# A third, SBUF-resident decay buffer for a selective scan, with decays made two parts ahead

## The chip, the cores and the metric

The kernel runs on one core of a Trainium2 chip. The metric is device time in microseconds (us) from the first to the last instruction of one launch; lower is better. Engines are named as in the profile: PE (TensorE matmul), PEld (its weight loads), DVE (VectorE), ACT (ScalarE), POOL (GpSimd), SP (SyncE, which issues almost all DMA here).

## The reference: what is computed

Input `x` is 8 images of 256 channels by 48x48 = 2304 positions, all float32. Two layers, each a residual on a group-normalised input.

Layer 0 compares all positions of an image: `pos` is normalised per position, `sim = pos @ pos.T`, the 16 largest similarities of each row go through a softmax, and the result is the weighted sum of the features of those 16 positions.

Layer 1 applies a selective-scan block twice (depth `d` = 0, 1), 512 channels by 16 states, over the 2304 positions in order:

```python
def step(h, inp):
    dt_t, B_t, C_t, x_t = inp
    dA = jnp.exp(dt_t[:, :, None] * A)
    h = h * dA + dt_t[:, :, None] * B_t[:, None, :] * x_t[:, :, None]
    y = jnp.einsum('bds,bs->bd', h, C_t)
    return (h, y)
```

`dA` is what this text calls a **decay**: one number per channel, state and position.

## The kernel before

Positions are cut in 6 chunks of T = 384. A **unit** is one chunk of one image at one depth: 8 x 6 x 2 = 96 units. A unit has 16 **steps**; a step covers 32 channels with their 16 states, laid out as 128 partitions by 4 state columns. A step has 2 **parts** of 2 states each. So there are 96 x 16 x 2 = 3072 parts, numbered `m`, and everything in the main loop hangs on that number. A part takes about 3 us.

For each part, in this order of the program:

- `carry(m - 1)` (L859, ACT) copies the last column of the previous part's states out to `h_st`, where that part was not one of POOL's.
- `decay` (L828, ACT) makes decays: two Exp instructions, 128x385 each (one column of zeros to restart the scan, then 384 positions), into the buffer that `decays(m)` names.
- on even parts, `make_bx(n + 2)` (L804, POOL) multiplies `BC` and `dtxr` into `bx` for the step two ahead, 128x1536; `pool_part(n - 1)` (L871, POOL) multiplies the states of the last step by C, for those parts that the table `SHARE` gives to POOL; `take_up` (ACT, or a memset of POOL) puts the carried states in `bx`.
- the hooks of the lists `between` and `behind`: projections, loads, normalisation of the units around this one. Each has a part number, relative to its unit, at which it is put into the queues. `load_in` (L590) loads one 128 KB tile `inw` of the input projection's weights, used by `in_proj` (L602) of the same number.
- `run_scan(m)` (L843, DVE) is one scan instruction over 770 columns. Its first input is the decays, its second is `bx`. Where POOL does the multiplication by C (part marked G in `SHARE`), the states are written over `bx`; where DVE does it, they are written over the decays, and a DVE multiply (L845) then takes decays and `BC` to `bx`.
- `sum_states` (L889, PE) later sums `bx` over the states into `y`.

Layer 0 of the next image runs interleaved with the scan, one slice of work a part (`ahead.go(m)`): similarity matmuls, DVE's top-16 (four instructions of about 2.5 us a block of 128 rows), ACT's exponentials into tiles `aT`, and at the end of a block `average` (L472) into `o`, with the residual `xr` loaded beside it (L474). Layer 0 of the first image runs alone, ahead of everything.

The order on each engine is the order of the program: it is written by hand, and each engine works its queue strictly in order. Waits are semaphores between engines.

The decay buffers of the kernel before are two PSUM tiles of two banks each. [...]

```python
    def decays(m):
        return banks[m % 2][:, 511 - T : 513 + T]
...
        carry(m - 1)
        decay(m + 1)
```

Of the kernel before, what the change touches and what calls it, by code (L numbers as in the profile page):

```python
# [8 lines left out]
F32 = mybir.dt.float32  # L9
# [6 lines left out]
P = 128  # L16
# [9 lines left out]
def tile_conv_preact(  # L26
# [19 lines left out]
    B, C, N = x.shape  # L46
# [4 lines left out]
    CB = C // P  # L51
    DB = DI // P
    NB = N // P
    T = 384
# [6 lines left out]
    HQ = 2  # L61
# [168 lines left out]
    def layer0(b, left, pool, ps0, alone):  # L230
# [3 lines left out]
        more = 2 if alone else 1  # L234
# [233 lines left out]

        def average(t):
            row = blocks[t]  # L470
            row["o"] = pool.tile([P, C], F32, tag="o", name=f"o_{b}_{t}", bufs=more)
            nc.scalar.activation(row["o"], row["po"], AF.Identity, scale=row["den"])  # L472
            row["xr"] = pool.tile([P, CB, P], F32, tag="xr", name=f"xr_{b}_{t}", bufs=more)
            nc.sync.dma_start(  # L474
                row["xr"], x[b, :, t * P : (t + 1) * P].rearrange("(k p) t -> p k t", p=P)
            )
# [9 lines left out]
        def finish(t):  # L486
# [15 lines left out]
            (-5, similar, 4), (-8, keep_similar, 0), (-5, keep_similar, 2), (24, turn_back), (18, weigh, 1),  # L502
            (17, weigh, 0), (1, top, 1), (-9, similar, 0), (-8, similar, 1), (-7, similar, 2),
            (22, average), (-6, similar, 3), (-7, keep_similar, 1), (-3, keep_similar, 3), (0, top, 0),
            (-3, keep_similar, 4), (15, turn, 1), (10, others, 4), (5, others, 0), (3, top, 2),
            (6, add_top), (11, invert), (5, others, 2), (17, turn, 2), (20, turn, 3),
# [18 lines left out]
    with tc.tile_pool(name="first", bufs=1) as pool0, tc.tile_pool(  # L525
        name="first_ps", bufs=1, space=PSUM
# [7 lines left out]
    with tc.tile_pool(name="setup", bufs=2) as setup:  # L534
        for d in range(DEPTH):
            for t in range(DC, DC + 1):
                dg = setup.tile([P, DB, P], F32, tag="dg", name=f"dg_{d}_{t}")
                for k in range(DB):
                    f = cw[:, d, k, t : t + 1] if t < DC else dpar[:, d, k : k + 1]
# [3 lines left out]
    keep = ctx.enter_context(tc.tile_pool(name="keep", bufs=2))  # L543
# [8 lines left out]
        nc.vector.memset(t[:, 0:1], NEVER)  # L552
    banks = [ps.tile([P, 1024], F32, tag=f"da{i}", name=f"da_{i}", bufs=1) for i in range(2)]

    def decays(m):
        return banks[m % 2][:, 511 - T : 513 + T]

    def mm(w, name):
        return ps.tile([P, 512], F32, tag="mm", name=name, bufs=3)[:, :w]
# [28 lines left out]
        unit["BC"].append(t)  # L588

    def load_in(unit, e):  # L590
        t = keep.tile([P, CB, P], F32, tag="inw", name=f"inw_{unit['u']}_{e}", bufs=4)
        nc.sync.dma_start(
            t, in_wT[unit["d"]].rearrange("(k p) e -> p k e", p=P)[:, :, e * P : (e + 1) * P]
        )
        unit["inw"][e] = t
# [168 lines left out]
    def silu_z(unit):  # L764
# [3 lines left out]
        for e in range(DB - 1):  # L768
# [11 lines left out]
             dt=[], dt_d={}, dtx_d={}, dtr={}, dtxr={}, bx={}, y={}, inw={}, dmat={}, taps={}, xi={}, cv={},  # L780
# [7 lines left out]
    def at(n):  # L788

        return units[n // STEPS], n % STEPS, n % STEPS // J  # L790
# [6 lines left out]
    def make_bx(n):  # L797


        if not 0 <= n < NSTEP:  # L800
            return
        unit, i, k = at(n)
        bx = keep.tile([P, Q, 1 + T], F32, tag="bx", name=f"bx_{n}", bufs=8)
        nc.gpsimd.tensor_tensor(  # L804
            bx[:, :, 1:], unit["BC"][0],
            unit["dtxr"][i].unsqueeze(1).to_broadcast([P, Q, T]), ALU.mult,
        )
        unit["bx"][i] = bx

    def take_up(n):  # L810

        if not 0 <= n < NSTEP:
            return
        unit, i, k = at(n)
        if unit["c"] == 0:
            nc.gpsimd.memset(unit["bx"][i][:, :, 0], 0.0)
        else:
            nc.scalar.copy(unit["bx"][i][:, :, 0], h_st[:, unit["d"], i])

    def decay(m):  # L820

        n, p = divmod(m, PARTS)
        if not 0 <= n < NSTEP:
            return
        unit, i, k = at(n)
        da = decays(m)
        for s in range(HQ):
            nc.scalar.activation(  # L828
                da[:, s * (1 + T) : (s + 1) * (1 + T)], unit["dtr"][i],
                AF.Exp, scale=A_sb[:, unit["d"], i, p * HQ + s : p * HQ + s + 1],  # L830
            )

    def run_scan(m):
        n, p = divmod(m, PARTS)
        if not 0 <= n < NSTEP:
            return
        unit, i, k = at(n)
        qs = slice(p * HQ, (p + 1) * HQ)
        bx = unit["bx"][i][:, qs]
        g = bx.rearrange("p q t -> p (q t)")  # L840
        da = decays(m)
        h = g if on_pool(unit, i, p) else da
        nc.vector.tensor_tensor_scan(h, da, g, 0.0, ALU.mult, ALU.add)  # L843
        if h is da:
            nc.vector.tensor_tensor(  # L845
                bx[:, :, 0:T], da.rearrange("p (q t) -> p q t", q=HQ)[:, :, 1:],
                unit["BC"][1][:, qs], ALU.mult,
            )

    def carry(m):  # L850

        n, p = divmod(m, PARTS)
        if not 0 <= n < NSTEP:
            return
        unit, i, k = at(n)
        if not on_pool(unit, i, p):
            h = decays(m).rearrange("p (q t) -> p q t", q=HQ)
            if unit["c"] + 1 < NCH:
                nc.scalar.copy(h_st[:, unit["d"], i, p * HQ : (p + 1) * HQ], h[:, :, T])  # L859

    def pool_part(n):

        if not 0 <= n < NSTEP:
            return
        unit, i, k = at(n)
        lo = [p for p in range(PARTS) if on_pool(unit, i, p)]
        if not lo:
            return
        qs = slice(lo[0] * HQ, (lo[-1] + 1) * HQ)
        g = unit["bx"][i][:, qs]  # L870
        nc.gpsimd.tensor_tensor(g[:, :, 0:T], g[:, :, 1:], unit["BC"][1][:, qs], ALU.mult)  # L871

    def carry_pool(n):

        if not 0 <= n < NSTEP:
            return
        unit, i, k = at(n)
        lo = [p for p in range(PARTS) if on_pool(unit, i, p)]
        if lo and unit["c"] + 1 < NCH:
            qs = slice(lo[0] * HQ, (lo[-1] + 1) * HQ)  # L880
            nc.scalar.copy(h_st[:, unit["d"], i, qs], unit["bx"][i][:, qs, T])
# [30 lines left out]
    def leave(unit, cb):  # L912
# [20 lines left out]
        (17, load_d, 2), (-17, tap, 1), (18, load_rep, "dtx", 13), (-8, times_x, 1), (19, gate, 1),  # L933
        (-22, normal), (1, load_rep, "dt", 3), (0, load_rep, "dtx", 4), (15, load_rep, "dt", 10), (6, load_rep, "dtx", 7),
        (10, load_rep, "dtx", 9), (12, load_rep, "dtx", 10), (20, load_rep, "dtx", 14), (11, gate, 0), (-29, spread_root),
        (-19, load_in, 5), (33, load_out), (-22, load_in, 0), (21, load_rep, "dt", 13), (-20, tap, 0),
        (-10, step_size, 1), (9, copy_z, 2), (-18, in_proj, 2), (2, load_rep, "dtx", 5), (10, sum_states, 0),
        (13, load_rep, "dt", 9), (29, gate, 2), (9, silu_z), (7, load_rep, "dt", 6), (19, load_rep, "dt", 12),
        (-6, load_rep, "dtx", 1), (-14, load_in, 7), (-30, root), (9, load_rep, "dt", 7), (4, load_d, 1),
        (-24, load_in, 3), (17, load_rep, "dt", 11), (14, load_rep, "dtx", 11), (-13, x_proj), (-17, load_in, 6),  # L940
        (-3, load_d, 0), (4, load_rep, "dtx", 6), (-4, load_rep, "dtx", 2), (-42, load_v),
    ]
    behind = [
# [1 line left out]
        (-8, load_rep, "dtx", 0), (-15, tap, 3), (-1, load_rep, "dt", 2), (-28, scale), (16, load_rep, "dtx", 12),  # L945
        (11, load_rep, "dt", 8), (8, in_proj, 6), (17, sum_states, 1), (-14, silu_x), (25, load_rep, "dt", 15),
        (-37, affine), (1, times_x, 2), (7, copy_z, 0), (8, load_rep, "dtx", 8), (-17, tap, 2),
        (-10, softplus), (-16, in_proj, 3), (3, load_rep, "dt", 4), (-29, load_in, 2), (6, in_proj, 7),
        (35, gate, 3), (-2, load_rep, "dtx", 3), (8, copy_z, 1), (40, leave, 1), (-3, times_x, 3),
        (22, load_rep, "dtx", 15), (-16, load_in, 4), (29, load_d, 3), (-37, mean), (-19, taps, 0),  # L950
        (-19, in_proj, 1), (-10, load_bc, 0), (33, sum_states, 3), (-30, root_end), (-9, times_x, 0),
        (-22, load_in, 1),
    ]
    inner, outer = {}, {}
    for w, unit in enumerate(units):
# [35 lines left out]
    for m in range(first, PARTS * NSTEP - HOOKS + last + 1):  # L991
        n, p = divmod(m, PARTS)
        carry(m - 1)
        decay(m + 1)
        if p == 0:
            make_bx(n + LEAD)
            pool_part(n - 1)
            take_up(n + 1)
        else:
            carry_pool(n - 1)  # L1000
        for f, unit, args in inner.get(m, ()):
            if f is load_v:
                ahead.finish(unit["b"])
            f(unit, *args)
        run_scan(m)
        for f, unit, args in outer.get(m, ()):
            f(unit, *args)
        ahead.go(m)
# [41 lines left out]
```

## Time and profile before

The time before is 9903.8 us (median of 2 runs, 9897.2 to 9910.4). The profiled execution spans 9897.1 us.

| engine | busy, us | share of the span | instructions |
|---|---|---|---|
| PE | 8000.3 | 81% | 36736 |
| DVE | 8956.8 | 90% | 7993 |
| ACT | 7322.2 | 74% | 15966 |
| POOL | 8943.3 | 90% | 3927 |

Read it in two stretches. In the first 515 us layer 0 of the first image runs alone: POOL is busy for 24.6 us of it and DVE for 242.4. In the rest, 9382 us, the scan runs with everything beside it, with DVE and POOL both busy for over nine tenths of each slice. A group's row gives the line, the engine, the output and inputs by name, the tile sizes, the count, then the busy time in us and the mean of one in ns, and last the idle time of the engine just before such an instruction with what ended it.

### The profile page before, as it was taken

Reading aid. Unit: us, or ns where it says so; the run is one execution under the profiler, and the core shown is the slowest. Engines: PE = TensorE matmul, PEld = TensorE weight load, DVE = VectorE, ACT = ScalarE, POOL = GpSimd, SP = SyncE. Lnnn points to the kernel's source line nnn. Section 1 sums busy time; section 2 is a strip of 40 time slices with the busy share of each in tenths; the row PEclk is TensorE's granted clock in tenths of the full one; section 3 lists DMA queues with packets and bytes.
Section 4 is the critical chain, followed back from the end, with each engine's and each line's share of the span. In section 5 each row is a group of like instructions: output and inputs, shape, how many; then the busy total and the mean of one; then the engine's idle time right before and its main releaser. Section 6 shows DMA issues by size and latency. Waiting matters only on the chain. (4 is left out here: it accounts for less than half of the span.)

```text
span 9897.1 us, 133780 instructions
## 1 busy us (share of the span) xinstructions
PE 8000.3 (81%) x36736; PEld 4388.5 (44%) x36736; DVE 8956.8 (90%) x7993; ACT 7322.2 (74%) x15966; POOL 8943.3 (90%) x3927
## 2 busy tenths in 40 slices
PE   8878887788878888788877888778887788866665
PEld 6644544444534454445444445344544444522222
DVE  4589998999989999899998999899998999988998
ACT  4477777778777877777877787777787778766766
POOL 0099999999989999899998999999998999999999
PEclk9989998899989998899988999889998899977777
DMA  1144445444444444444454444444445444444544
GB/s 32 37 133 126 134 130 152 124 132 129 136 142 131 129 134 137 140 126 133 130 148 128 130 128 134 144 132 125 135 128 152 121 133 127 138 136 129 145 138 122
DMA packets 1243503, 1271.37 MB, mean 128 GB/s; under 512 B 266592, under 2 KB 1215840, under 8 KB 1242752
## 3 DMA queue, kind: packets, MB, share of 16 engines
q1 hardware_dynamic: 1230496, 1262.45, 44.7%
q8 instruction: 293, 4.80, 0.2%
q14 instruction: 458, 3.75, 0.1%
q10 hardware_dynamic: 12256, 0.36, 0.1%
HBM read 1048.94 MB, written 212.86 MB: 127 GB/s over the span
## 5 line engine op out<-in xcount | busy, mean ns | idle before, releaser
L804 POOL TENSOR_TENSOR bx<-BC,dtxr 128x1536 f32<-128x1536 f32 x1536 | 5298.4, 3453 | 115.6 <-PE y L889 59.8
L828 ACT ACTIVATE da<-dtr,A_sb 128x385 f32<-128x385 f32 x6144 | 3591.0, 585 | 871.6 <-DVE bx L843 558.0
L843 DVE TENSOR_TENSOR_SCAN bx<-da,bx 128x770 f32<-128x770 f32 x2040 | 3521.8, 1746 | 190.5 <-ACT da L828 151.4
L871 POOL TENSOR_TENSOR bx<-bx,BC 128x1536 f32<-128x1536 f32 (+1 forms) x1320 | 3303.6, 2503 | 217.5 <-DVE bx L843 205.4
L843 DVE TENSOR_TENSOR_SCAN da<-da,bx 128x770 f32<-128x770 f32 x1032 | 1808.8, 1753 | 193.4 <-ACT da L828 149.0
L602 PE MATMUL pe<-vn,inw 128*128 128x384 f32 (+1 forms) x3072 | 1258.9, 543 | 394.1 <-DVE xr L924 87.0
L399 PE MATMUL psim<-pos 128*128 128x512 f32 (+1 forms) x2880 | 1370.8, 608 | 183.5 <-ACT sim L408 74.7
L465 PE MATMUL po<-feat,aT 128*128 128x256 f32 x5184 | 1364.0, 412 | 13.8 <-ACT aT L454 7.6
L889 PE MATMUL y<-bx,sel 128*32 128x384 f32 x12288 | 1221.2, 533 | 44.2 <-POOL bx L871 37.9
L465 PEld LDWEIGHTS po<-feat,aT 128*128 128x128 f32 x5184 | 1029.8, 205 | 361.9 <-issue 113.9
L845 DVE TENSOR_TENSOR bx<-da,BC 128x768 f32<-128x768 f32 x1032 | 988.8, 958 | 35.5
L602 PEld LDWEIGHTS pe<-vn,inw 128*128 128x128 f32 x3072 | 590.1, 206 | 902.6 <-issue 191.2
L399 PEld LDWEIGHTS psim<-pos 128*128 128x128 f32 x2880 | 552.8, 206 | 818.8 <-issue 470.8
L889 PEld LDWEIGHTS y<-bx,sel 128*32 128x32 f32 x12288 | 394.1, 118 | 856.6 <-issue 725.0
L702 DVE SCALAR_TENSOR_TENSOR xc<-pe,cw,xc 128x384 f32<-128x384 f32 x1152 | 695.7, 611 | 42.8 <-ACT xc L694 15.7
L732 PE MATMUL pd<-dbl,dtp_sb 16*128 16x384 f32 x768 | 424.3, 668 | 342.0 <-ACT dt L741 209.0
L859 ACT COPY h_st<-da 128x2 f32<-128x2 f32 x832 | 131.7, 158 | 686.4 <-DVE bx L845 680.0
L454 ACT ACTIVATE aT<-pt 128x512 f32<-128x512 f32 (+1 forms) x720 | 388.1, 548 | 245.9 <-PE pt L446 239.8
L445 PE MATMUL pt<-ident,sim 128*128 128x128 f32 x2592 | 539.6, 291 | 33.7 <-DVE v L666 17.6
L907 PE MATMUL pw<-z,ow 128*128 128x384 f32 x1536 | 531.5, 499 | 15.0 <-DVE v L666 7.0
L437 ACT ACTIVATE rest<-left,three 128x512 bf16<-128x512 f32 (+1 forms) x720 | 467.0, 670 | 59.7 <-DVE left L422 59.7
L446 PE MATMUL pt<-minus,rest 128*128 128x128 bf16 x2592 | 491.6, 225 | 3.2 <-ACT rest L437 3.2
(146 smaller groups left out, 9766.8 us busy)
## 6 DMA issues: line engine op xcount, KB each, us to landing
dtxr<-dtx_d SPq DMA_DIRECT2D x6144, 48.0 KB, 1.8
dtr<-dt_d SPq DMA_DIRECT2D x6144, 48.0 KB, 1.8
BC<-bc_d SPq DMA_DIRECT2D x768, 192.0 KB, 3.7
inw<-in_in_wT_dram SPq DMA_DIRECT2D x768, 128.0 KB, 2.2
dtx_d<-dtx SPq DMA_DIRECT2D x384, 192.0 KB, 2.0
dt_d<-dt SPq DMA_DIRECT2D x384, 192.0 KB, 2.2
ow<-in_out_wT_dram SPq DMA_DIRECT2D x96, 512.0 KB, 4.0
dmat<-diag SPq DMA_DIRECT2D x384, 64.0 KB, 2.3
```

The lines of the kernel that those rows point to most:

```text
L399: nc.tensor.matmul(pm, pos[:, k, t * P : (t + 1) * P], pos[:, k, c0 : c0 + w], start=(k == 0), stop=(k == CB - 1),)
L445: nc.tensor.transpose(pt[:, q], row["sim"][:, r], ident)
L465: nc.tensor.matmul(row["po"], aT[:, m % PT, :], feat[:, m, :], start=(m == 0), stop=(m == NB - 1))
L602: nc.tensor.matmul(pe, w[:, k], unit["vn"][:, k, lo:], start=(k == 0), stop=(k == CB - 1))
L702: nc.vector.scalar_tensor_tensor(unit["xc"][e], unit["pe"][e][:, k : k + T], cw[:, unit["d"], e, k : k + 1], unit["xc"][e], ALU.mult, ALU.add,
L804: nc.gpsimd.tensor_tensor(bx[:, :, 1:], unit["BC"][0], unit["dtxr"][i].unsqueeze(1).to_broadcast([P, Q, T]), ALU.mult,)
L828: nc.scalar.activation(da[:, s * (1 + T) : (s + 1) * (1 + T)], unit["dtr"][i], AF.Exp, scale=A_sb[:, unit["d"], i, p * HQ + s : p * HQ + s ...
L843: nc.vector.tensor_tensor_scan(h, da, g, 0.0, ALU.mult, ALU.add)
L845: nc.vector.tensor_tensor(bx[:, :, 0:T], da.rearrange("p (q t) -> p q t", q=HQ)[:, :, 1:], unit["BC"][1][:, qs], ALU.mult,)
L871: nc.gpsimd.tensor_tensor(g[:, :, 0:T], g[:, :, 1:], unit["BC"][1][:, qs], ALU.mult)
L889: nc.tensor.matmul(y[j * G : (j + 1) * G, :], sel, unit["bx"][k * J + j][:, q, 0:T], start=False, stop=True, skip_group_check=True,)
L907: nc.tensor.matmul(pw, unit["ow"][:, k, cb * P : (cb + 1) * P], unit["z"][k], start=(k == 0), stop=(k == DB - 1),)
```

## The change

The scan gets a third decay buffer. PSUM is full, so it is an SBUF tile, `room`, of 128 x 770 float32 = 3080 bytes a partition. Parts with `m % 3 == 2` use it; the others use the two PSUM buffers as before. With three buffers ACT makes the decays of part `m + 2` in part `m`, where it made those of `m + 1`.

The room for it comes from three places, 1 KB a partition each: layer 0's tiles `o` and `xr` lose their own buffers and take turns with `aT`, and `inw` has 3 buffers where it had 4. The part numbers of six of the eight `load_in` hooks (all but 4 and 7) are set anew for that.

```diff
-            row["o"] = pool.tile([P, C], F32, tag="o", name=f"o_{b}_{t}", bufs=more)
+            row["o"] = pool.tile([P, C], F32, tag="aT", name=f"o_{b}_{t}", bufs=2 * more)
...
-            row["xr"] = pool.tile([P, CB, P], F32, tag="xr", name=f"xr_{b}_{t}", bufs=more)
+            row["xr"] = pool.tile([P, CB, P], F32, tag="aT", name=f"xr_{b}_{t}", bufs=2 * more)
...
+    room = keep.tile([P, HQ * (1 + T)], F32, tag="room", name="room", bufs=1)
+
     def decays(m):
-        return banks[m % 2][:, 511 - T : 513 + T]
+        return room if m % 3 == 2 else banks[m % 3][:, 511 - T : 513 + T]
...
-        t = keep.tile([P, CB, P], F32, tag="inw", name=f"inw_{unit['u']}_{e}", bufs=4)
+        t = keep.tile([P, CB, P], F32, tag="inw", name=f"inw_{unit['u']}_{e}", bufs=3)
...
-        (-19, load_in, 5), (33, load_out), (-22, load_in, 0), (21, load_rep, "dt", 13), (-20, tap, 0),
+        (-15, load_in, 5), (33, load_out), (-22, load_in, 2), (21, load_rep, "dt", 13), (-20, tap, 0),
...
-        (-24, load_in, 3), (17, load_rep, "dt", 11), (14, load_rep, "dtx", 11), (-13, x_proj), (-17, load_in, 6),
+        (-24, load_in, 1), (17, load_rep, "dt", 11), (14, load_rep, "dtx", 11), (-13, x_proj), (4, load_in, 6),
...
-        (-10, softplus), (-16, in_proj, 3), (3, load_rep, "dt", 4), (-29, load_in, 2), (6, in_proj, 7),
+        (-10, softplus), (-16, in_proj, 3), (3, load_rep, "dt", 4), (-29, load_in, 0), (6, in_proj, 7),
...
-        (-22, load_in, 1),
+        (-20, load_in, 3),
...
-        decay(m + 1)
+        decay(m + 2)
```

## The prediction

> **What bounds the kernel now.** I began with the page's busy times and slices, then the costliest groups, then the chain of waits and one line's spread of durations.
>
> ```profile
> PE 8000.3 (81%) x36736; PEld 4388.5 (44%) x36736; DVE 8956.8 (90%) x7993; ACT 7322.2 (74%) x15966; POOL 8943.3 (90%) x3927
> ...
> DVE  4589998999989999899998999899998999988998
> ACT  4477777778777877777877787777787778766766
> POOL 0099999999989999899998999999998999999999
> ```
>
> After the first two slices DVE and POOL are both at nine tenths. By stretches: from 515 us on (9382 us), DVE is busy 8956.8 - 242.4 = 8714 us and idle 668; POOL is busy 8943.3 - 24.6 = 8919 and idle 463. ACT has 2290 us to spare. So two engines stand near saturation side by side, and neither can take on 500 us without moving the end.
>
> ```profile
> L804 POOL TENSOR_TENSOR bx<-BC,dtxr 128x1536 f32<-128x1536 f32 x1536 | 5298.4, 3453 | 115.6 <-PE y L889 59.8
> L828 ACT ACTIVATE da<-dtr,A_sb 128x385 f32<-128x385 f32 x6144 | 3591.0, 585 | 871.6 <-DVE bx L843 558.0
> L843 DVE TENSOR_TENSOR_SCAN bx<-da,bx 128x770 f32<-128x770 f32 x2040 | 3521.8, 1746 | 190.5 <-ACT da L828 151.4
> L871 POOL TENSOR_TENSOR bx<-bx,BC 128x1536 f32<-128x1536 f32 (+1 forms) x1320 | 3303.6, 2503 | 217.5 <-DVE bx L843 205.4
> L843 DVE TENSOR_TENSOR_SCAN da<-da,bx 128x770 f32<-128x770 f32 x1032 | 1808.8, 1753 | 193.4 <-ACT da L828 149.0
> ...
> L845 DVE TENSOR_TENSOR bx<-da,BC 128x768 f32<-128x768 f32 x1032 | 988.8, 958 | 35.5
> ```
>
> POOL's time is two lines of two-input multiplies, all of whose operands (`BC`, `dtxr`, `bx`) are in SBUF. DVE's largest item is the scan, 3072 of 1.75 us; its decays are in PSUM and `bx` is in SBUF.
>
> ```profile
> ACT da L828 <- DVE bx L843: 558.0, 680, 3.5
> ...
> DVE bx L843 <- ACT da L828: 151.4, 186, 3.1
> DVE da L843 <- ACT da L828: 149.0, 61, 5.7
> ```
>
> In the waits (total us, times, longest) DVE loses 300 us to late decays. That is the change's target, and its ceiling on DVE.
>
> ```profile
> L804 POOL TENSOR_TENSOR bx<-BC,dtxr x1536: 3407/3448/3547, 508.4 to 9872.3; 128x1536 f32<-128x1536 f32 x192
> ...
> L843 DVE TENSOR_TENSOR_SCAN bx<-da,bx x2040: 1697/1749/1762, 517.7 to 9882.3; 128x770 f32<-128x770 f32 x186
> ```
>
> These two (minimum/median/maximum ns of one line's instructions) are the reading that decides me: the scan varies by 4% and the multiply by 4%, though the two engines overlap nearly all the time. Today they do not disturb each other.
>
> **What the Trainium skill says.** "SBUF — State Buffer", section "Who interferes with whom": POOL's SBUF ports are VectorE's second pair. A VectorE instruction with at most one SBUF input, outside the two-port modes, does not contend with GpSimd; one "with two SBUF inputs contends with a GpSimd instruction that reads SBUF". Section "SBUF: two separate sides": the pair is an exclusive lock, held for the whole instruction, and the later one blocks. The trace of before agrees with the first half: every scan and every L845 has one PSUM and one SBUF input, and the spreads above show no disturbance. It shows no large VectorE instruction with two SBUF inputs, so the second half is untested here. "ScalarE: Activation LUTs", section "Step-by-step: what each stage is for", calls PSUM the faster destination for ScalarE. The Exp to PSUM takes 585 ns; a 128x384 activation to SBUF takes 508 (Silu, L710, no pointer operand) to 663 (L694, two): no difference to charge.
>
> **The change part by part.**
>
> *Third buffer, decays two ahead.* The decays of part m+2 go where those of m-1 were, so they wait for scan m-1, just as decay(m+1) did with two buffers: ACT's 558 + 116 us of waiting on DVE at L828 stay. What improves is that DVE finds the result a part (3 us) sooner. It removes at most 300 us of DVE idle. POOL's 463 us of idle includes 205 on scans (L871), which can shrink too. Without any other effect the gain is at most 300 and, since POOL would then stand at 515 + 8919 = 9434 plus its other waits of about 260 = 9690, I take 200.
>
> *`room` in SBUF.* A third of the scans, 1024, now have both inputs in SBUF, and so do a third of L845, 344, since `SHARE` repeats every 16 parts and 16 is no multiple of 3. Their own length hardly moves. What they hold, in time in which POOL may not read: 1024 x 1.75 + 344 x 0.958 = 1792 + 330 = 2122 us. Bounds: 0 if they do not exclude each other at all, 2122 if fully.
> POOL, fully excluded: 8919 + 2122 = 11,041, after 515: 11,556 with no idle at all; with all of today's idle kept, 12,019.
> DVE, fully excluded: a scan that arrives at a random moment waits for the rest of the running POOL instruction. Sum of count x length squared, halved, over 9382 us: (1536 x 3.453² + 720 x 3.184² + 600 x 1.685² + 384 x 1.005²)/2 = 13,850; / 9382 = 1.48 us each. 1024 x 1.48 = 1510. An L845 follows its own scan at once, while a POOL instruction has been waiting: either DVE keeps the port (0) or it waits a whole POOL instruction (mean 2.77 us); half of that, 344 x 1.4 = 480. DVE: 8714 + 1510 + 480 = 10,704, plus the 368 us of its idle that decays don't cause, plus 515 = 11,587.
> So the floors of the two engines meet at about 11,560 to 11,590. Two engines that pass one lock to and fro do not both run without idle; I add 60 and take 11,650.
> Queued behind a blocked scan on DVE are the top-16 instructions, `taps` and `gate`, and ACT waits for the scan to refill the buffer; behind a blocked L804 or L871 on POOL are `times_x`, and PE's sums of states (L889). The step of lead that `make_bx(n + 2)` gives softens this and does not create time on either engine.
>
> *`o` and `xr` in `aT`'s two buffers.* `o` is made at part 22 of a block, after all five `aT` are in use; `turn_back` and `finish` read them at 24, and the next block's first `aT` comes at 15 + 16 = 31. Seven parts, 20 us, cover it: 0. The load of `xr` may now wait for ACT's last `aT`, made a part or two before: 0.
>
> *`inw` with three buffers.* The same 768 loads. `load_in` 6 stands at part 4, and its buffer is the one that `in_proj` 7 reads at part 6: SP waits there up to two parts, with the loads of `dtr` for step 5 and `dtxr` for step 6 queued behind it, both used at part 8. That leaves about a part, 3 us, against 1.8 us to land. Between 0 and 96 x 3 = 290 us; nearest row, POOL's present waits of 25 us for `dtxr`. I take 0, as the lock leaves slack elsewhere.
>
> Sum: 11,650; the gain of decays two ahead does not show, because it removes idle of DVE where POOL and the lock set the pace.
>
> **Rivals.**
> 1. *No contention:* the scan's second read does not trouble POOL. 9904 - 200 = 9700 (between 9600 and 9850), on the faster side. For it: the trace has nothing that shows the lock. Against: the skill states it for exactly this pair of operands.
> 2. *Partial contention:* the scan takes 1746 ns for 770 columns, 2.27 ns each, against 1.25 for L845, so it wants the second port at most every other cycle. If the port is shared by cycles, POOL loses about half: 9434 + 1061 + some 200 of idle = 10,700. Against it: "not a bandwidth split".
> 3. *Starvation:* if POOL's next instruction takes the port ahead of a waiting scan, DVE gets it only when POOL runs out of work, and POOL then idles for the scan and for DVE's arrears. Full exclusion makes (11,590 - 515) / 512 = 21.6 us of three steps with their two such scans; one more half-length of a POOL instruction (1.4 us) for the arrears of each three steps gives 512 x 1.4 = 720, so about 12,400.
>
> **How the numbers follow.** Full exclusion 0.72 at 11,650 (11,400 to 12,100); partial 0.10 at 10,700; starvation 0.08 at 12,400; none 0.10 at 9700. The range leaves out no contention and the far ends of partial and starvation: 10,600 to 12,200. No contention divides about evenly at 9706, the 2% line: faster 0.05, same 0.05, slower 0.90.
>
> **What would show it.** Right: L843 no longer within 4% but with a third of its instructions, those that read `room`, at some 3 us (wait inside them) or with as much idle ahead of them; L804 and L871 with a mean 0.5 to 1.0 us longer, or gaps of that size; the sum of busy and blocked time on POOL near 11,000 us; DVE's wait for L828 down from 300 us to under 100. Wrong: L804 still at 3.45 us and reading-`room` scans at 1.7 us, which would leave rival 1; only POOL longer and by under 0.4 us, rival 2; SP waiting on PE at L592 for over 300 us with POOL's waits on `dtxr` grown alike, which would put the loss in the loads and not in the port.

## The result and the profile after

The changed kernel takes 11,904.5 us (median) against 9903.8 before: ratio 1.202, 95% interval 1.199 to 1.205. It is slower by a fifth. Line numbers of the changed kernel are two higher from L558 on: the scan is L845, the multiply by C L847, POOL's two multiplies L806 and L873, the Exp L830.

The page's busy times and slices, after:

```profile
PE 8612.6 (72%) x36736; PEld 4652.4 (39%) x36736; DVE 11018.2 (93%) x7993; ACT 7273.8 (61%) x15966; POOL 10328.9 (87%) x3927
...
DVE  4599999999999999999999999899998999999999
ACT  4466666666666665666666666666656666655554
POOL 0299999999999988989999899899998999898898
```

The instruction counts are those of before, and yet DVE is busy for 2061 us more and POOL for 1386 us more (PE too, for 612 us; more on that at the end of the experiments). Equal counts with more busy time mean that single instructions became longer. The costliest groups, by tile, tell which:

```profile
L806 POOL TENSOR_TENSOR bx<-BC,dtxr 128x1536 f32<-128x1536 f32 x1536 | 5903.8, 3845 | 494.0 <-PE y L891 256.3
L873 POOL TENSOR_TENSOR bx<-bx,BC 128x1536 f32<-128x1536 f32 (+1 forms) x1320 | 3768.1, 2855 | 495.9 <-DVE bx L845 402.6
...
L845 DVE TENSOR_TENSOR_SCAN bx<-da,bx 128x770 f32<-128x770 f32 x1360 | 2351.1, 1742 | 49.5 <-POOL bx L818 47.5
...
L845 DVE TENSOR_TENSOR_SCAN bx<-room,bx 128x770 f32<-128x770 f32 x680 | 1982.7, 2916 | 6.4 <-POOL bx L818 4.3
...
L845 DVE TENSOR_TENSOR_SCAN room<-room,bx 128x770 f32<-128x770 f32 x344 | 1114.5, 3240 | 50.0 <-POOL bx L818 24.2
L847 DVE TENSOR_TENSOR bx<-room,BC 128x768 f32<-128x768 f32 x344 | 1103.6, 3208 | 11.8
```

Scans that read `da`, in PSUM, have kept their 1.74 us. Scans of the same size that read `room` take 2.92 and 3.24 us, and the multiply that reads `room` 3.21 us in place of 0.96. The last figures show that DVE hardly idles ahead of a scan any more: it no longer waits for ACT, but its instructions take longer.

The spread of one line's durations (minimum/median/maximum ns), in the changed kernel:

```profile
L845 DVE TENSOR_TENSOR_SCAN bx<-da,bx x1360: 1691/1745/1764, 524.3 to 11883.1; 128x770 f32<-128x770 f32 x195
...
L845 DVE TENSOR_TENSOR_SCAN bx<-room,bx x680: 1734/2764/4914, 528.5 to 11887.5; 128x770 f32<-128x770 f32 x170
```

At its fastest a scan from `room` is about as fast as one from PSUM (1734 against 1691). What is added runs from nothing to 3.2 us: never more than one POOL instruction (3.45 us). One stretch in order of time shows it happen. First DVE, then POOL; columns are start, duration (both us), engine, line and operands:

```profile
5000.41 4.35 DVE L845 TENSOR_TENSOR_SCAN room<-room,bx 128x770 f32<-128x770 f32 x1
5004.80 3.74 DVE L847 TENSOR_TENSOR bx<-room,BC 128x768 f32<-128x768 f32 x1
```

```profile
4999.65 3.51 POOL L806 TENSOR_TENSOR bx<-BC,dtxr 128x1536 f32<-128x1536 f32 x1
5003.08 4.64 POOL L873 TENSOR_TENSOR bx<-bx,BC 128x1536 f32<-128x1536 f32 x1
5007.68 4.15 POOL L806 TENSOR_TENSOR bx<-BC,dtxr 128x1536 f32<-128x1536 f32 x1
```

The scan starts at 5000.41 while L806 runs to 5003.16. It ends at 5004.76, which is 1.6 us after L806's end: it did nearly all of its own work, 1.74 us, after POOL was through. L873, started at 5003.08, ends at 5007.72, some 3 us after the scan's end: now POOL waited. The multiply started at 5004.80 and ends at 5008.54, 0.8 us after L873. Then L806 from 5007.68 takes 4.15. The two engines take turns, one whole instruction each, and the wait is recorded as part of the busy time.

The rest of the trace goes the same way. Of the 1024 scans that read `room`, 794 took over 0.3 us longer than a scan from PSUM. In all of these POOL was at work when they began, and all but one ended 1.61 to 1.63 us after the end of the instruction that POOL was at. Of the 344 multiplies, 329 were held up, and all of them ended 0.81 to 0.82 us after the end of POOL's instruction. No large POOL multiply overtook one that waited; the one exception is a `dtx` multiply (L754) that began 10 ns after the scan did. POOL's memsets (L818, L677), which have no input, did pass.

### The profile page after: what moved, and what is told of

Read it like the earlier page. It is cut to its first block, busy times and chain, and to the rows that moved or that the text cites. A ratio compares the mean times of both kernels' runs of the same rounds, so it can differ in the third digit from the quotient of the medians.

```text
span 11903.0 us, 134307 instructions
## 1 busy us (share of the span) xinstructions
PE 8612.6 (72%) x36736; PEld 4652.4 (39%) x36736; DVE 11018.2 (93%) x7993; ACT 7273.8 (61%) x15966; POOL 10328.9 (87%) x3927
## 5 line engine op out<-in xcount | busy, mean ns | idle before, releaser
L806 POOL TENSOR_TENSOR bx<-BC,dtxr 128x1536 f32<-128x1536 f32 x1536 | 5903.8, 3845 | 494.0 <-PE y L891 256.3
L873 POOL TENSOR_TENSOR bx<-bx,BC 128x1536 f32<-128x1536 f32 (+1 forms) x1320 | 3768.1, 2855 | 495.9 <-DVE bx L845 402.6
L830 ACT ACTIVATE da<-dtr,A_sb 128x385 f32<-128x385 f32 x4096 | 2395.3, 585 | 1020.9 <-DVE bx L845 422.7
L845 DVE TENSOR_TENSOR_SCAN bx<-da,bx 128x770 f32<-128x770 f32 x1360 | 2351.1, 1742 | 49.5 <-POOL bx L818 47.5
L830 ACT ACTIVATE room<-dtr,A_sb 128x385 f32<-128x385 f32 x2048 | 1150.7, 611 | 1521.3 <-DVE bx L847 650.2
L845 DVE TENSOR_TENSOR_SCAN bx<-room,bx 128x770 f32<-128x770 f32 x680 | 1982.7, 2916 | 6.4 <-POOL bx L818 4.3
L465 PE MATMUL po<-feat,aT 128*128 128x256 f32 x5184 | 1439.5, 429 | 97.9 <-ACT aT L454 94.4
L465 PEld LDWEIGHTS po<-feat,aT 128*128 128x128 f32 x5184 | 1091.0, 217 | 484.4 <-ACT aT L454 153.5
L845 DVE TENSOR_TENSOR_SCAN da<-da,bx 128x770 f32<-128x770 f32 x688 | 1203.3, 1749 | 74.7 <-issue 23.8
L845 DVE TENSOR_TENSOR_SCAN room<-room,bx 128x770 f32<-128x770 f32 x344 | 1114.5, 3240 | 50.0 <-POOL bx L818 24.2
L847 DVE TENSOR_TENSOR bx<-room,BC 128x768 f32<-128x768 f32 x344 | 1103.6, 3208 | 11.8
L704 DVE SCALAR_TENSOR_TENSOR xc<-pe,cw,xc 128x384 f32<-128x384 f32 x1152 | 696.3, 611 | 75.5 <-ACT xc L696 47.2
L847 DVE TENSOR_TENSOR bx<-da,BC 128x768 f32<-128x768 f32 x688 | 659.6, 959 | 23.8
L754 POOL TENSOR_TENSOR dtx<-dt,xc 128x384 f32<-128x384 f32 x384 | 619.4, 1613 | 18.7 <-ACT dt L743 16.6
```

The costliest lines, as they stand in the source:

```text
L465: nc.tensor.matmul(row["po"], aT[:, m % PT, :], feat[:, m, :], start=(m == 0), stop=(m == NB - 1))
L704: nc.vector.scalar_tensor_tensor(unit["xc"][e], unit["pe"][e][:, k : k + T], cw[:, unit["d"], e, k : k + 1], unit["xc"][e], ALU.mult, ALU.add,
L754: nc.gpsimd.tensor_mul(dtx, unit["dt"][k], unit["xc"][k])
L806: nc.gpsimd.tensor_tensor(bx[:, :, 1:], unit["BC"][0], unit["dtxr"][i].unsqueeze(1).to_broadcast([P, Q, T]), ALU.mult,)
L830: nc.scalar.activation(da[:, s * (1 + T) : (s + 1) * (1 + T)], unit["dtr"][i], AF.Exp, scale=A_sb[:, unit["d"], i, p * HQ + s : p * HQ + s ...
L847: nc.vector.tensor_tensor(bx[:, :, 0:T], da.rearrange("p (q t) -> p q t", q=HQ)[:, :, 1:], unit["BC"][1][:, qs], ALU.mult,)
```

## The experiments

All runs are compared with the kernel before on the same chip, 9897 to 9908 us. An edit can move the line numbers of a run by one or two, so go by the tiles. They were to tell apart two theories. **Port:** the loss comes from DVE instructions with two SBUF inputs and POOL's reads of SBUF shutting each other out (contention, below). **Loads:** it comes from making room in SBUF, that is from SP's waits on three `inw` buffers and on `xr` in `aT`'s buffers. SP's longest waits in the changed kernel (total us, times, longest) speak for the second theory too, since in the kernel before SP waited 74 us for PE at the `inw` load and 26 us, for a DMA, at `xr`'s:

```profile
SPq L594 <- PE pe L604: 1205.3, 214, 16.9
...
SPq L474 <- PE po L465: 566.0, 122, 82.4
```

**e1, contention of the scans alone, on the kernel before.** Parts with `m % 3 == 2` compute other states here, with values of `BC` in the place of decays.

```diff
-        nc.vector.tensor_tensor_scan(h, da, g, 0.0, ALU.mult, ALU.add)
+        src = unit["BC"][1].rearrange("p q t -> p (q t)")[:, 0 : HQ * (1 + T)] if m % 3 == 2 else da
+        nc.vector.tensor_tensor_scan(h, src, g, 0.0, ALU.mult, ALU.add)
```

> The kernel before, with its two PSUM buffers, its lead of one part and its loads; only the scans of every third part take the 770 columns of the first input from BC, in SBUF, in place of the decays in PSUM (so those parts compute other states; all decays are still made). Port theory: a scan with two SBUF inputs waits for the running GpSimd instruction. In the changed kernel 1024 such scans cost 1307 us more than 1.75 us each, and DVE sets the pace, so 9904 + 1200 (1000 to 1400) = 11,100, with these scans at 2.7 to 3.2 us. Loads theory (the loss comes from the input-weight loads and the shared aT buffers, which are as before here): 9904 within 1%, all scans at 1.75 us.

11,282 us, ratio 1.139 (1.137 to 1.141). Nothing else was changed, and the loss is two thirds of that of the changed kernel, inside the range of the port theory. The groups of the scan show the same pair as above, without `room`:

```profile
L844 DVE TENSOR_TENSOR_SCAN bx<-da,bx 128x770 f32<-128x770 f32 x1360 | 2352.4, 1743 | 64.2 <-POOL bx L816 36.9 <-ACT da L828 22.2 <-POOL bx L804 4.4
L844 DVE TENSOR_TENSOR_SCAN bx<-BC,bx 128x770 f32<-128x770 f32 x680 | 2014.2, 2962 | 4.9 <-POOL bx L816 4.9
```

`BC` is written by DMA, long before, so it isn't ACT's writing of `room` that slows the scan. One group, scans of `BC` over the decays, took 3.39 us, a little above the expected 2.7 to 3.2.

**e2, the multiplies too.** Those parts' multiply takes `BC` by `BC`.

```diff
-                bx[:, :, 0:T], da.rearrange("p (q t) -> p q t", q=HQ)[:, :, 1:],
-                unit["BC"][1][:, qs], ALU.mult,
+                bx[:, :, 0:T],
+                unit["BC"][0][:, qs] if m % 3 == 2 else da.rearrange("p (q t) -> p q t", q=HQ)[:, :, 1:],
+                unit["BC"][1][:, qs], ALU.mult,
```

> As the run before, and the 344 DVE multiplies of every third part take both inputs from SBUF too (BC by BC, so their product is another one). Port theory: another 344 x 2.25 us = 774 us as in the changed kernel, so 9904 + 1950 = 11,850 (11,600 to 12,100), and the multiplies at 3 us or more. Loads theory: 9904 within 1%.

11,990 us, ratio 1.210 (1.209 to 1.212): 708 us more than e1, from 344 instructions, which now take 3.04 us on average:

```profile
L846 DVE TENSOR_TENSOR bx<-BC,BC 128x768 f32<-128x768 f32 x344 | 1046.7, 3043 | 11.8
```

This is already above the changed kernel. Two SBUF inputs on a third of the parts are enough for all of its loss, with no new buffer and no new load order.

**e3, the changed kernel without contention.** Parts of `room` compute other states: their scan and multiply read the PSUM decays of the part after. POOL's parts among them don't read `room` at all, so ACT refills it somewhat more freely than in the changed kernel.

```diff
-        nc.vector.tensor_tensor_scan(h, da, g, 0.0, ALU.mult, ALU.add)
+        src = banks[0][:, 511 - T : 513 + T] if m % 3 == 2 else da
+        nc.vector.tensor_tensor_scan(h, src, g, 0.0, ALU.mult, ALU.add)
...
-                bx[:, :, 0:T], da.rearrange("p (q t) -> p q t", q=HQ)[:, :, 1:],
+                bx[:, :, 0:T], src.rearrange("p (q t) -> p q t", q=HQ)[:, :, 1:],
```

> The changed kernel with all its buffers, loads and decays two ahead; only the scans of room's parts read the PSUM decays of the part after (already made), and so do the multiplies behind them (so those parts compute other states; ACT still fills room). No DVE instruction has two large SBUF inputs. Port theory: every scan back at 1.75 us, POOL's multiply back at 3.45, and 9700 to 10,000, lower than before if decays two ahead bring what was predicted (about 200). Loads theory: stays above 11,500.

10,210 us, ratio 1.031 (1.029 to 1.032). 1695 us of the 2001 are gone, and POOL's L806 and the scans of `room`'s parts are back at their old lengths:

```profile
L806 POOL TENSOR_TENSOR bx<-BC,dtxr x1536: 3412/3449/3553, 510.5 to 10177.9; 128x1536 f32<-128x1536 f32 x192
...
L846 DVE TENSOR_TENSOR_SCAN room<-da,bx x344: 1701/1751/1762, 535.6 to 10167.5; 128x770 f32<-128x770 f32 x172
```

The port is the main cause, but the rest is 3% slower than before where I expected it between 2% faster and 1% slower. The idle of ACT before the Exp, by what ended it, shows what is new (first the kernel before, then e3):

```profile
  DVE bx L843: 558.0, 680
...
  DMA dtr<-dt_d: 7.5, 8
```

```profile
  DMA dtr<-dt_d: 616.4, 219
  DVE bx L846: 433.3, 411
```

ACT now stands for 616 us at Exp instructions whose `dtr` (the step sizes of which they make decays) has not landed, and everything behind them in its queue stands too. DVE's wait for decays is 296 us in e3, what it was before. But that is mostly the experiment's own doing: 279 of the 296 us stand ahead of the scans of `room`'s parts, which read the decays of the part after and so have one part of lead where the changed kernel gives them two. For those of them that write to `room`:

```profile
DVE room L846 <- ACT da L830: 134.5, 70, 6.9
```

So how much of the 3% the changed kernel would have without contention stays open.

**e4, the loads alone.** The changed kernel without `room`: two PSUM buffers and `decay(m + 1)`, but `o` and `xr` in `aT`'s buffers, three `inw` buffers and the new hooks.

```diff
-        return room if m % 3 == 2 else banks[m % 3][:, 511 - T : 513 + T]
+        return banks[m % 2][:, 511 - T : 513 + T]
...
-        decay(m + 2)
+        decay(m + 1)
```

> The changed kernel without room: two PSUM buffers and decays one part ahead as before, but o and xr in aT's buffers, three inw buffers and the new load hooks. Port theory: 9900 to 10,050, the cost of SP's waits alone (in the changed kernel SP waited 1205 us for inw and 566 us for xr, mostly hidden). Loads theory: above 11,500.

9971 us, ratio 1.007 (1.005 to 1.008). Making the room costs 63 us by itself, although SP waits 739 us for `inw` and 328 for `xr`. The loads theory falls as the explanation of the whole; a few per cent remain to be shared out.

**e5, one part ahead, with contention.** Only the lead of the changed kernel is undone.

```diff
-        decay(m + 2)
+        decay(m + 1)
```

> The changed kernel, with room, but decay(m + 1) in place of decay(m + 2). If two parts ahead is a gain (as predicted, up to 300 us of DVE's waits on decays): slower than the changed kernel, 11,950 to 12,200. If it is a loss (each decay stands a part earlier in ACT's order and is stuck for its dtr load, 534 us of ACT's waits in the changed kernel): faster, 11,650 to 11,850.

11,761 us, ratio 1.188 (1.186 to 1.190): 144 us faster than two ahead. The change's aim, decays earlier, costs time here.

**e6, one part ahead, without contention.** As e3 with `decay(m + 1)` and `banks[1]`, the tile of the part before, in place of `banks[0]`; other states are computed in the same parts.

> The changed kernel with decay(m + 1), and the scans of room's parts, with the multiplies behind them, take the PSUM tile of the part before in place of room (so those parts compute other states). No contention. If two ahead costs time through ACT's waits for dtr, this lies well under the 10,210 us of the same kernel with two ahead: 9800 to 9950. If three buffers or the loads cost it: about 10,200.

9995 us, ratio 1.010 (1.008 to 1.011), somewhat above the expected span, and 215 us under e3. The 215 us are not a clean price of two ahead, as e3 and e6 differ in the tile that stands in for `room`: e3 has the 279 us above, and in e6 DVE waits 185 us ahead of its scans for ACT's `carry` (L862), which it does in no other of these runs. For the same reason the 23 us by which e6 lies above e4 don't say what a third buffer with one part ahead is worth.

```profile
DVE room L846 <- ACT h_st L862: 101.0, 56, 4.3
...
DVE bx L846 <- ACT h_st L862: 83.7, 62, 4.3
```

**e7, e3 with the loads eased.**

```diff
-            nc.sync.dma_start(
+            nc.scalar.dma_start(
                 row["xr"], x[b, :, t * P : (t + 1) * P].rearrange("(k p) t -> p k t", p=P)
...
-        (-24, load_in, 1), (17, load_rep, "dt", 11), (14, load_rep, "dtx", 11), (-13, x_proj), (4, load_in, 6),
+        (-24, load_in, 1), (17, load_rep, "dt", 11), (14, load_rep, "dtx", 11), (-13, x_proj),
...
-        (-10, softplus), (-16, in_proj, 3), (3, load_rep, "dt", 4), (-29, load_in, 0), (6, in_proj, 7),
+        (-10, softplus), (-16, in_proj, 3), (3, load_rep, "dt", 4), (-29, load_in, 0), (6, in_proj, 7), (6, load_in, 6),
```

> The changed kernel without contention (as in the run that gave 10,210 us, decays two ahead), and with the loads eased: inw 6 is loaded behind in_proj 7 of part 6, and xr's load is issued by ACT, behind the average that has already waited for po. If SP's stalls on inw and xr make dtr late: 9750 to 9950. If dtr is late because its own load hooks stand at part 2k - 5 and are now used at 2k - 2: about 10,150.

9944 us, ratio 1.004 (1.003 to 1.006): easing two kinds of load takes 266 us off. ACT's wait for `dtr` falls from 616 to 333 us, and the stand-in is that of e3. So nearly half of ACT's waiting for `dtr` came about because SP, which works its queue in order (its 15,898 DMA instructions come in one order in the changed kernel and in e5), stood at `inw` 6 and at `xr` with the `dtr` loads behind them.

**e8, e7 with every `dt` load hook one part earlier** (`(5, load_rep, "dt", 5)` becomes `(4, load_rep, "dt", 5)`, and so on for all 16).

> As the run before, and all dt loads one part earlier, so that a dtr has three parts to land as with one part ahead. If lateness of dtr is the whole cost of two ahead, this shows what a third buffer without contention is worth: 9600 to 9800, under the kernel before. If it stays at or over 9900, two ahead brings nothing even with its loads in time.

10,004 us, ratio 1.011 (1.009 to 1.012): a miss, slower than e7. Of SP's longest waits in e8:

```profile
SPq L578 <- ACT h_st L884: 452.3, 242, 5.2
...
SPq L578 <- ACT da L830: 281.7, 204, 4.6
```

A load that is issued earlier finds its `dtr` buffer, one of three, still in use by the Exp of three steps before, and SP stands there instead. ACT's wait for `dtr` did fall, to 264 us; that SP's new waits are what made e8 slower was not tested. More `dtr` buffers were not tried; the change itself had to collect its 3 KB of SBUF from three places.

**e9 and e10, loads eased with contention,** two parts and one part ahead.

> The changed kernel, contention and all, with the loads eased: inw 6 loaded behind in_proj 7 of part 6, and xr's load issued by ACT behind the average. If the 266 us that easing saved without contention are saved here too: 11,640 (11,550 to 11,750). If contention hides SP's stalls, as was predicted: 11,900 within 1%.

> As the run before, with decay(m + 1) in place of decay(m + 2). If dtr's lateness is what makes two ahead cost time, easing the loads takes most of it away and the two kernels lie within 0.7% of each other; if two ahead costs by itself, this one is again 140 us faster, near 11,500.

e9: 11,763 us, ratio 1.189 (1.187 to 1.190), 141 us under the changed kernel, between the two expectations. e10: 11,748 us, ratio 1.187 (1.185 to 1.188), within 0.2% of e9, and of e5, so easing the loads helps only with two parts ahead. With its loads in time, two ahead neither costs nor gains. ACT's wait for `dtr` ahead of the Exp, in the changed kernel, in e9 and in e10:

```profile
  DMA dtr<-dt_d: 534.1, 132
...
  DMA dtr<-dt_d: 93.6, 70
...
  DMA dtr<-dt_d: 7.4, 5
```

Two ahead does what it was to do: DVE waits 24 us for decays in e9 and 143 in e10. But from 515 us on DVE is busy 10,799 us in e9 and 10,695 in e10: about what it no longer waits for decays it now waits inside its instructions, all of it in the scans and multiplies that read `room` (4224 us against 4118).

No version with a third buffer came out under 9904 us. Those without contention carry the waits of their stand-ins, so what a third buffer in PSUM would bring was not measured.

One more rival: the clock that PE was granted is lower in the slower kernels, 0.84 in the changed kernel and 0.89 before, and PE is busy longer. Nothing here points to it as the cause: scans from PSUM take 1.74 us in both, POOL's undisturbed multiplies 3.45, and the waits for PE do not follow the clock (POOL waits 250 us for `y` in e3 at 0.88, and 109 in e5 at 0.83). Why the clock is lower stays open.

## Why the prediction was right

The time, 11,904 us, lies in the range, on the side and by the cause that was forecast; the sum was 254 us short. From 515 us on, DVE is busy 10,778 us and idle 610 in the changed kernel, by the table of stretches, which with the 515 is the whole span. DVE has the least idle of all engines, so the forecast's DVE sum can be gone through term by term. (Columns of the line: stretch, length, then PE, PEld, DVE, ACT and POOL busy.)

```profile
515.00:11903.00 11388.00, 8162.80 (x34648) 4338.09 (x34647) 10777.73 (x7724) 7049.32 (x15505) 10310.48 (x3839) 0.83 0.40 110
```

- *Scans wait for the rest of a POOL instruction, 1024 x 1.48 = 1510 us.* Measured: (1982.7 + 1114.5) - 1024 x 1.748 = 1307 us, 1.28 each. Right in kind, 16% high.
- *Multiplies wait, half a POOL instruction each, 344 x 1.4 = 480 us.* Measured: 1103.6 - 344 x 0.959 = 774 us, 2.25 each. This is the term that was mis-sized. I had both ends, nothing and a whole instruction (2.77), and took the middle. By the count above 329 of the 344 wait out a POOL instruction, mostly a long one (the median duration is 3746 ns): POOL queued up behind the scan, and its turn comes first. The two terms together are 2081 against 1990. One was 203 us too high and the other 294 too low, so the nearness of the sum is in part luck.
- *DVE's other idle, 368 us, and 60 added for the handing to and fro.* Measured 610 in all. The 300 us of waiting for decays did go, down to 27 us at L845, but other waits grew by more: DVE for PE's `y` from 118 to 175 us, for ACT at the taps (L704) from 16 to 47. The lock was to leave slack for the loads, and it did not: e9 gives 141 us back.
- *POOL's floor, 8919 + 2122 = 11,041 us.* POOL was blocked for 10,310 - 8919 = 1392 us only, and its idle rose from 463 to 1078: only 1080 of POOL's large multiplies (L806, L873, L754) became longer by over 0.15 us, though DVE took 1368 turns. L806 is longer by 0.39 us on average and L873 by 0.35, where the sign named 0.5 to 1.0. That the two floors met was a coincidence of the estimate. In the changed kernel DVE is the nearer to full; in e1 it is POOL (idle 593 us from 515 us on, DVE 672).
- *Two ahead gains 200 us at most and doesn't show.* It is no gain, but it doesn't come to nothing either: it costs 144 us (e5). I looked at who waits for a decay and not at what a decay waits for: `dtr` is used one part sooner while its loads keep their hooks, and the same edit put two new stalls in front of them on SP. Once the loads are eased, the cost is gone, and the gain still isn't there, for the reason forecast: the lock takes it back (e9 and e10).
- *`o` and `xr` in `aT`, 0; `inw` with three buffers, 0 of 0 to 290 us.* Alone they cost 63 us (e4). With decays two ahead, easing them gave back 141 us with contention (e9) and 266 without (e7 against e3; there the stand-in makes DVE feel a late decay more). The stall at `load_in` 6 had been named, as a bound. For `xr` I looked only at ACT's last `aT` and at the block after, and missed that its buffer must also be read out by PE (`weigh`, L465): 566 us of SP's waits.

Of the rivals, no contention fell with e1, and partial contention with the stretch and the counts above, in which each side waits for the end of the other's instruction. Starvation fell with the same counts and with the maxima: no scan took over 5.02 us, less than one POOL instruction and itself. The sign that was to mean "the loss is in the loads" did appear (SP over 300 us at the `inw` load, POOL's wait on `dtxr` from 25 to 171 us), beside the signs of the port; such a sign shows that a cause is there, not that it is the only one.

The Trainium skill's "SBUF — State Buffer", section "Who interferes with whom", carried the forecast, and the runs agree with it: two SBUF inputs on DVE against reads of POOL cost 1375 us in e1, and the same scans from PSUM cost none. "ScalarE: Activation LUTs", section "Step-by-step: what each stage is for", has PSUM as the faster destination, and the trace agrees: the Exp takes 585 ns to PSUM and 611 to `room`. Over the 2048 Exps to `room` that is 53 us, on an engine that is idle for 4339 us from 515 us on.

What stays open: why e7, free of contention and with the loads eased, is still 0.4% above the kernel before. ACT's remaining 333 us for `dtr` are one likely place; the other is the stand-in, as 172 of the 188 us that DVE waits for decays in e7 stand at `room`'s parts. Neither was tried by itself.

## What to carry to other kernels

Before moving an operand from PSUM to SBUF, count the SBUF inputs of every DVE instruction that reads it, the multiplies behind the scan included. If POOL is busy with SBUF reads, charge each instruction that then has two the rest of a POOL instruction, and a whole one where it stands right behind another such instruction. A buffer more lets the producer run ahead only if its own inputs come earlier too: trace what the earlier instruction waits for, through the queue that loads it. A new wait on an in-order DMA queue is paid by whatever stands behind it, so look for it by the names of the loads that come late, not by the load that waits.

## What the runs showed that I had not expected

- The wait for the port is inside the recorded duration, on both engines: DVE's busy time rose by 2061 us with the same instructions, and a page that shows 93% busy hides it. The same instruction on other tiles (1742 against 2916 ns) gives it away, and so does the spread of one line.
- The engines take turns: the one that waited goes next. A DVE instruction right behind another contended one therefore waits for a whole POOL instruction (2.25 us on average), longer than a scan, which comes at any moment of one (1.28 us).
- A third of the scans and multiplies with two SBUF inputs cost 21% in e2, while DVE and POOL were each at 90% before; small POOL instructions are hit as well (in the changed kernel the 128x3 one of L170 takes 442 ns on average, 196 before, though the median stays at 198).
